# Where the last stage's inputs are stored: a ternary feed-forward kernel whose final reload of x gets more places in SBUF

## The chip, the cores and the metric

The kernel runs on one core of a Trainium2 chip. The metric is the device time of one execution in microseconds (us), the median of the runs of a kernel. A profiled execution has a time of its own and a span, from the first to the last instruction in the trace; instants below ("at 1038.7") are microseconds from the span's start. MB are millions of bytes; a block of x or of the output is 1.049 MB.

## The reference

x has 128 samples of 64 channels by 512 positions, in fp32 (16.78 MB). Each sample picks one of 200 matrices of 64 by 64; the picked matrix mixes the channels. Then a two-layer feed-forward network with ternary weights runs over the 512 positions of each of the 8192 rows, its output y is rounded to 15 levels with one scale for the whole tensor, and x is added.

```python
c = einsum('bct,bcd->bdt', x, weights[conditions])
W1q, W2q = ternarize(W1), ternarize(W2)     # alpha * sign(W) where |W| > 0.05 * max|W|
h = gelu(c @ W1q.T + b1)                    # 512 -> 2048
y = h @ W2q.T + b2                          # 2048 -> 512
scale = max(abs(y)) / 7 + 1e-8              # one number, over all of y
out = x + clip(round(y / scale), -7, 7) * scale
```

The scale needs the largest |y| of all blocks, so no output can be written before the last y is there.

## The kernel before

The rows are cut into 16 blocks (NB) of four pairs of samples: 128 partitions by 4 by 512, in fp32. A block n goes through 16 steps hc, one for each 128 of the 2048 hidden units. In a step, TensorE does eight matmuls of layer 1 into `ph` (`layer1`) and eight of layer 2 into the four accumulators `py0` to `py3` (`layer2`), the latter for the step two earlier (LAG). Activations are split in a high and a low fp32r part, so that each product is two matmuls. Between the layers ScalarE does the gelu into `hf` and rounds it to the high part, and VectorE subtracts to get the low part (`bend`, `split`).

The ternary weights rest in SBUF as fp8, `w1t` and `w2t`, one buffer each. GpSimd widens one step's share of them at a time to fp32r: `widen1` for the next step's layer 1, `widen2` for the layer 2 of the step before (`w1f`, `w2f`, three buffers each, pool `wide`). GpSimd also issues the gathers of the picked matrices (`fetch`, L172) and copies them into the block diagonals `diag` (`place`, L184), for the block after.

The kernel opens with the work on the weights: SP loads W1, x block 0 and W2; VectorE finds the largest |W1|, TensorE spreads it over the partitions by a transpose (`tops_delta_w`), VectorE makes masks and signs, TensorE transposes them. Until the first real matmul, TensorE does 64 matmuls `idle` on a tile of ones. Block 0 runs its two layers one after the other, in step with the preparation of W2 (L538 to L656); from block 1 the loop at L661 runs as above.

Storage: the pool `big` has 21 buffers of 8 KB a partition, for x blocks, their two parts, raw weights, masks, `w1t`, `w2t`, and the y of each block, which `result` (L433) takes out of PSUM. When the last block runs, 15 y are held, and the 16th gets a buffer when it is done.

All engines keep the program's order (`InOrder`, L43), and so does SP's queue of loads: a load that waits for its buffer holds up all loads after it. Loads of x are issued as two halves of 0.524 MB. The last stage needs x again. `load_x` is called for x0 and x1 in the last block (L675), for x2 at its end (in the buffer of `w1t`), and for x3 and x4 after it (L703; in the last block's parts). When the main loop's pools are closed (L727), a pool `last` takes their place with three x buffers for x5, x6 and x7, and x8 to x15 go into buffers of x and y that the last stage sets free (L734).

The last stage itself (L732 to L748), by half blocks: ScalarE rounds y into an int8 `q` (three buffers), VectorE writes q times scale plus x over y, GpSimd issues the write to `out`. Ahead of it stand the largest |y| of the last block and the scale (L708 to L724): for each j, VectorE takes y out of PSUM (`result`) and reduces it (`largest`); then one transpose spreads the maximum.

Of the kernel before, what the change touches and what calls it, by code (L numbers as in the profile page):

```python
# [25 lines left out]
F32 = mybir.dt.float32  # L26
BF16 = mybir.dt.bfloat16
F32R = mybir.dt.float32r
# [26 lines left out]
def tile_cond_ternary_ffn(  # L55
# [30 lines left out]
    const = ctx.enter_context(tc.tile_pool(name="const", bufs=1))  # L86
    big = ctx.enter_context(tc.tile_pool(name="big", bufs=21))
    gather = ctx.enter_context(tc.tile_pool(name="gather", bufs=2 * PAIRS))
    main = ctx.enter_context(ExitStack())
    hid = main.enter_context(tc.tile_pool(name="hid", bufs=3))  # L90
    wide = main.enter_context(tc.tile_pool(name="wide", bufs=3))
    ps_c = ctx.enter_context(tc.tile_pool(name="ps_c", bufs=2, space=PSUM))
# [5 lines left out]

    def load_x(n, pool=big, tag="big"):
        xt = pool.tile([P, PAIRS, T], F32, tag=tag, name=f"xt_{n}")  # L100
        for h in range(2):
            js = slice(h * PAIRS // 2, (h + 1) * PAIRS // 2)
            sp.dma_start(out=xt[:, js, :], in_=x_blk[n][:, js, :])
        return xt

    first = big.tile([P, 3, B], F32, tag="big", name="first")
    cond_i = first[:, 0, :].bitcast(I32)
    sp.dma_start(out=cond_i, in_=conditions.partition_broadcast(P))  # L110
# [8 lines left out]
    x_next = load_x(0)  # L119
    b1n = const.tile([NH, P], F32)  # L120
    sp.dma_start(out=b1n, in_=b1.rearrange("(k p) -> k p", p=P))
# [14 lines left out]
    make_identity(nc, ident_f)  # L136
    ones_b = const.tile([P, T], BF16)
    pool.memset(ones_b, 1.0)
# [10 lines left out]
    rows = const.tile([P, B // 2], I32)  # L149
    cond_f = first[:, 1, :]  # L150
    dve.tensor_copy(cond_f, cond_i)
    wrap = first[:, 2, :]
    dve.tensor_scalar(wrap, cond_f, 0.0, float(S), ALU.is_lt, ALU.mult)
    dve.tensor_tensor(cond_f, cond_f, wrap, ALU.add)
    dve.tensor_scalar(cond_f, cond_f, 0.0, float(S - 1), ALU.max, ALU.min)
    cond_2 = cond_f.rearrange("p (j two) -> p j two", two=2)
    for h in range(2):
        half = slice(h * C, (h + 1) * C)
        dve.tensor_scalar(
            rows[half, :], cond_2[half, :, h], float(C), chan_f[half, :], ALU.mult, ALU.add  # L160
        )
    table = weights.rearrange("s c d -> (s c) d")


    diag = []
    for j in range(PAIRS):
        wd = const.tile([P, P], F32, tag=f"diag{j}", name=f"diag{j}")
        pool.memset(wd, 0.0)
        diag.append(wd)

# [13 lines left out]
    def place(j, wg):  # L184
        for h in range(2):
            half = slice(h * C, (h + 1) * C)
            pool.tensor_copy(diag[j][half, h * D : (h + 1) * D], wg[half, :])

# [8 lines left out]
    def mix(xt, j, pc):  # L197

        for c in range(NT):
            pe.matmul(  # L200
                out=pc[:, c, :],
                lhsT=xt[:, j, c * P : (c + 1) * P],
                rhs=diag[j],
                start=True,
                stop=True,
            )
# [6 lines left out]

    w1t = big.tile([P, NH, NT, P], F8, tag="big", name="w1t")
    w2t = big.tile([P, NH, T], F8, tag="big", name="w2t")

    def spread(top1, out):

        wide_top = const.tile([P, P], F32, tag="wide_top", name=f"wide_{out.name}")
        dve.tensor_copy(wide_top, top1.to_broadcast([P, P]))  # L220
        tops = ps_c.tile([P, P], F32, tag="pc", name=f"tops_{out.name}")
        pe.transpose(tops, wide_top, ident_f)
        return tops

    def thresholds(w, top):

        top1 = const.tile([P, 1], F32, name=f"top1_{w}")
        dve.tensor_reduce(top1, top, AX.X, ALU.max)
        delta = const.tile([P, 1], F32, name=f"delta_{w}")
        tops = spread(top1, delta)  # L230
        yield
        dve.tensor_reduce(delta, tops, AX.X, ALU.max)
        dve.tensor_scalar(delta, delta, THRESHOLD, None, ALU.mult)
        minus = const.tile([P, 1], F32, name=f"minus_{w}")
        dve.tensor_scalar(minus, delta, -1.0, None, ALU.mult)
        yield delta, minus
# [44 lines left out]
    def flat(w):  # L281
        return w.rearrange("p a b -> p (a b)")
# [14 lines left out]

    idle = ps_h.tile([P, T], F32, tag="ph", name="idle")
    for _ in range(64):
        pe.matmul(out=idle, lhsT=ones_b[:, :P], rhs=ones_b, start=True, stop=True)  # L300
    for g in range(NG):
# [18 lines left out]

    find = thresholds("w1", top_1)
    next(find)
# [19 lines left out]
    def count1(g, number, first, final):  # L342
        for i in range(WCH // T):
            pe.matmul(
                out=number,
                lhsT=ones_b[:, :P],
                rhs=tern1[g][:, 0, i * T : (i + 1) * T],
                start=(first and i == 0),
                stop=(final and i == WCH // T - 1),
            )  # L350
# [34 lines left out]
    def widen1(n, hc):  # L385

        w = wide.tile([P, NT, P], F32R, tag="w1f", name=f"w1f_{n}_{hc}")
        pool.tensor_copy(w, w1t[:, hc])
        wide1[n, hc] = w

    def widen2(n, hc):
        w = wide.tile([P, T], F32R, tag="w2f", name=f"w2f_{n}_{hc}")
        pool.tensor_copy(w, w2t[:, hc])
        wide2[n, hc] = w
# [130 lines left out]
    def alpha_2():  # L525
# [10 lines left out]
        alpha[2] = alpha_of("w2", both[:, 0:1], both[:, 1:2])  # L536

    widen1(0, 0)  # L538

# [41 lines left out]
    fetched = []  # L581
    find = thresholds("w2", top_2)
    made = {}
# [35 lines left out]
    for hc in range(5, NH):  # L619
# [5 lines left out]
        behind(hc)  # L625
    turned = turn2(0, 1, signs2[0][:, 1, :])
    widen2(0, 0)
    widen2(0, 1)
# [9 lines left out]
    for hc in range(NH - LAG):  # L638
# [13 lines left out]
        if 8 <= hc < 8 + NG:  # L652
            sum2(hc - 8)
    cond[1] = two_next
    widen1(1, 0)
    widen2(0, NH - LAG)  # L656


    steps = [(n, hc) for n in range(NB) for hc in range(NH)]
    again = []  # L660
    for s in range(NH, len(steps)):  # L661
        n, hc = steps[s]
        if s + 1 < len(steps):
            widen1(*steps[s + 1])
        widen2(*steps[s + 1 - LAG])
        if n + 1 < NB:
            if hc == 0:
                x_next = load_x(n + 1)
                two_next = parts(n + 1)
                fetched = []  # L670
            if 2 <= hc < 2 + PAIRS:
                fetched.append(fetch(n + 1, hc - 2))
            if 7 <= hc < 7 + PAIRS:
                place(hc - 7, fetched[hc - 7])
        if n == NB - 1 and hc in (2, 3, NH - 1):  # L675
            again.append(load_x(len(again)))
        ph = ps_h.tile([P, BLK], F32, tag="ph", name=f"ph_{n}_{hc}")
        layer1(n, hc, ph)
        bend(
            n,  # L680
            hc,
            ph,
            [hid.tile([P, BLK], F32R, tag=f"h{k}", name=f"h{k}_{n}_{hc}") for k in range(2)],
            hid.tile([P, BLK], F32, tag="hf", bufs=2, name=f"hf_{n}_{hc}"),
        )
        if n + 1 < NB and 8 <= hc < 8 + PAIRS:
# [14 lines left out]
    n = NB - 1  # L701
    widen2(n, NH - 1)
    for _ in range(2):  # L703
        again.append(load_x(len(again)))
    dve.tensor_reduce(
        ymax[:, NB, 0:1], ymax[:, : NB - 1].rearrange("p n j -> p (n j)"), AX.X, ALU.max
    )
    for j in range(PAIRS):  # L708
        for hc in range(NH - 1 - LAG, NH):
            layer2(n, hc, [j])  # L710
        result(n, j)
        largest(n, j)

# [5 lines left out]
    scale = const.tile([P, 1], F32, name="scale")  # L719
    tops = spread(ymax1, scale)  # L720
    dve.tensor_reduce(scale, tops, AX.X, ALU.max)
# [4 lines left out]

    main.close()  # L727
    last = ctx.enter_context(tc.tile_pool(name="last", bufs=3))
    for _ in range(3):
        again.append(load_x(len(again), last, "xt"))  # L730
    AHEAD = len(again)
    for n in range(NB):  # L732

        while len(again) < min(AHEAD + 3 * n // 2, NB):  # L734
            again.append(load_x(len(again)))
        xf = again[n].rearrange("p j t -> p (j t)")
        yf = ys[n].rearrange("p j t -> p (j t)")
        for h in range(2):
            half = slice(h * PAIRS * T // 2, (h + 1) * PAIRS * T // 2)
            js = slice(h * PAIRS // 2, (h + 1) * PAIRS // 2)  # L740


            q = last.tile([P, PAIRS * T // 2], I8, tag="q", name=f"q_{n}_{h}")
            act.activation(q, yf[:, half], AF.Identity, scale=inverse)
            dve.scalar_tensor_tensor(
                yf[:, half], q, scale, xf[:, half], ALU.mult, ALU.add
            )
            pool.dma_start(out=out_blk[n][:, js, :], in_=ys[n][:, js, :])  # L748

# [33 lines left out]
```

## Time and profile before

| | us |
|---|---|
| median of 3 runs (range) | 1110.41 (1109.86 to 1111.0) |
| profiled execution | 1111.39 |
| its span | 1109.5 |
| TensorE busy | 1024.4 (92% of the span) |
| VectorE, ScalarE, GpSimd busy | 398.7, 471.2, 474.1 |
| DMA moved | 62.01 MB |

The shares are means over three stages with different limits: the opening until about 72, the blocks until 1035.5, where TensorE is busy nearly all the time, and the last stage, where TensorE has nothing to do. A change to the last stage is to be read from the rows of that stretch.

### The profile page before, as it was taken

To read this page: it belongs to the slowest core of one execution; us is meant where nothing else is said; L and a number is where in the kernel's file an instruction comes from. 1 tells how busy PE (TensorE), PEld (TensorE's weight loads), DVE (VectorE), ACT (ScalarE), POOL (GpSimd) and SP (SyncE) were. 2 spreads that over 40 slices of the span, in tenths; PEclk is the share of its full clock that TensorE was granted. 3 is DMA by queue.
4 is the path that set the end of the run, shared out by engine and by line. 5 is a ranking of instruction groups with operands and counts; after the bars stand their busy time and mean duration, and the time that the engine had idled before them with its cause. 6 is when DMAs were issued, how large, how long until landed. Compare 5 with 4: busy or idle time off the path is not lost.

```text
span 1109.5 us, 13261 instructions
## 1 busy us (share of the span) xinstructions
PE 1024.4 (92%) x4832; PEld 839.9 (76%) x4832; DVE 398.7 (36%) x545; ACT 471.2 (42%) x648; POOL 474.1 (43%) x757
## 2 busy tenths in 40 slices
PE   8989999999999999999999999999999999999300
PEld 4768788888888888888888888888888888888200
DVE  6965323232322323232322323232323223231753
ACT  6855333434344343343343433434333334333551
POOL 3756435343443535343444435353434435333331
PEclk9999999999999999999999999999999999999755
DMA  9113100100101000100101000100101000021899
GB/s 331 71 39 114 43 1 6 38 6 1 40 4 40 5 1 6 38 5 1 42 2 40 4 1 6 38 6 1 43 1 41 3 1 5 1 77 38 320 415 362
DMA packets 28672, 62.01 MB, mean 56 GB/s; under 512 B 2736, under 2 KB 2880, under 8 KB 28608
## 3 DMA queue, kind: packets, MB, share of 16 engines
q1 hardware_dynamic: 21952, 42.28, 11.0%
q0 software_dynamic: 6656, 18.88, 4.4%
q8 instruction: 39, 0.64, 0.2%
q14 instruction: 25, 0.20, 0.1%
HBM read 44.38 MB, written 16.78 MB: 55 GB/s over the span
## 4 chain that ended last, share of the span: by engine, by line
PE 88%; DMA 4%; DVE 3%; issue 2%; POOL 1%; ACT 1%; SPq 0%; POOLq 0%; ACTq 0%; DVEq 0%
PE py L51 42%; PE ph L51 41%; PE pc L51 5%; DMA out<-y 3%; DMA nat<-in_L_ffn_W 1%; DVE tern L51 1%; DMA xt<-in_x 1%; DVE y L51 1%; POOL diag L51 0%; PE pt L51 0%; POOL out L51 0%; DVE ymax L51 0%; ACT ring L51 0%; ACT h L51 0%; DVE x L51 0%
## 5 line engine op out<-in xcount | busy, mean ns | idle before, releaser
L51 PE MATMUL py<-w2f,h 128*128 128x512 f32 x2048 | 516.9, 394 | 2.8 <-ACT ring L51 1.9
L51 PE MATMUL ph<-x,w1f 128*128 128x512 f32 (+1 forms) x2056 | 507.1, 389 | 3.3 <-POOL w1f L51 3.3
L51 PEld LDWEIGHTS ph<-x,w1f 128*128 128x128 f32 x2056 | 384.1, 188 | 84.5 <-POOL w1f L51 4.9
L51 PEld LDWEIGHTS py<-w2f,h 128*128 128x128 f32 x2048 | 378.5, 188 | 85.6 <-DVE y L51 5.6
L51 ACT ACTIVATE hf<-ph,b1t,alpha_w 128x512 f32<-128x512 f32 x240 | 187.2, 780 | 554.7 <-PE ph L51 554.7
L51 DVE TENSOR_TENSOR h<-hf,h 128x512 fp32r<-128x512 f32 x240 | 166.1, 692 | 650.8 <-ACT h L51 650.8
L51 POOL CAST w2f<-w2t 128x512 fp32r<-128x512 fp8e4 x256 | 184.9, 723 | 358.3 <-PE py L51 347.4
L51 POOL CAST w1f<-w1t 128x512 fp32r<-128x512 fp8e4 x256 | 163.5, 639 | 192.5 <-PE ph L51 179.1
L51 ACT CAST h<-hf 128x512 fp32r<-128x512 f32 x240 | 148.8, 620 | 7.6
L51 PEld LDWEIGHTS pc<-diag,xt 128*128 128x128 f32 x512 | 66.2, 191 | 4.5
L51 POOL DMA_INDIRECT wg<-in_L_cond_weights,rows x64 | 62.8, 982 | 13.1 <-issue 5.3
L51 PE MATMUL pc<-diag,xt 128*128 128x128 f32 x512 | 67.0, 274 | 0.0
L51 DVE SCALAR_TENSOR_TENSOR y<-q,scale,xt 128x1024 f32<-128x1024 int8 x32 | 39.4, 1281 | 26.3 <-DMA xt<-in_x 25.0
L51 ACT ACTIVATE q<-y,inverse 128x1024 int8<-128x1024 f32 x32 | 36.0, 1145 | 29.4 <-DVE y L51 19.9
L51 DVE TENSOR_TENSOR x<-pc,x 128x512 fp32r<-128x512 f32 x64 | 43.5, 683 | 9.1 <-ACT x L51 9.1
L51 POOL DMA_DIRECT2D out<-y x32 | 23.3, 728 | 54.4 <-DVE y L51 38.7
L51 DVE SCALAR_TENSOR_TENSOR y<-py,alpha_w,b2b 128x512 f32<-128x512 f32 x64 | 43.8, 743 | 0.7 <-PE py L51 0.5
L51 DVE TENSOR_REDUCE ymax<-y 128x1 f32<-128x512 f32 x64 | 39.6, 676 | 0.1
L51 ACT CAST x<-pc 128x512 fp32r<-128x512 f32 x64 | 37.1, 581 | 3.9 <-PE pc L51 3.9
L51 POOL COPY diag<-wg 64x64 f32<-64x64 f32 x128 | 33.8, 264 | 8.2 <-DMA wg<-in_L_cond_weights,rows 4.4
L51 DVE TENSOR_REDUCE top<-nat 128x1 f32<-128x2048 f32 x8 | 18.2, 2280 | 3.9 <-DMA nat<-in_L_ffn_W 3.9
L51 PE MATMUL idle<-ones_b 128*128 128x512 bf16 x64 | 16.4, 425 | 2.2 <-POOL ones_b L51 2.2
(73 smaller groups left out, 171.9 us busy)
## 6 DMA issues: line engine op xcount, KB each, us to landing
xt<-in_x SPq DMA_DIRECT2D x64, 512.0 KB, 4.9
out<-y POOLq DMA_DIRECT2D x32, 512.0 KB, 13.1
nat<-in_L_ffn_W SPq DMA_DIRECT2D x8, 1024.0 KB, 13.1
wg<-in_L_cond_weights,rows POOLq DMA_INDIRECT x64, 2.4
b2b<-in_L_ffn_b SPq DMA_DIRECT2D x1, 256.0 KB, 13.5
first<-in_itok_B SPq DMA_DIRECT2D x1, 64.0 KB, 3.5
b1n<-in_L_ffn_b SPq DMA_DIRECT2D x1, 8.0 KB, 11.1
```

Of the source, the lines that this page charges most:

```text
L51: return lambda *args, **kw: self._tc.keep_in_program_order(make(*args, **kw))
```

## The change

It gives the reload of x more places, and frees what it needs for that:

- `last` and the closing of the main pools are gone. One pool `half` of six half-size buffers (4 KB a partition) replaces `hid` and `wide`: one each for `w1f`, `w2f` and `hf`, of two slots each, and three for the two parts of h. After the main loop the six take the halves of x7, x8 and x9.
- `w1f` and `w2f` have two slots from block 1 on instead of three. For block 0 the slots are in `big`: four of `w1f0` and four of `w2f0`. The last `widen2` goes into a slot of `w1f`.
- `big` has 22 buffers. The last y takes none: it gets its alpha and bias in place in PSUM, is reduced there and rounded from there, and its output is written over x15.
- x0, x1, x2 are loaded at steps 0, 1 and 2 of the last block. x3 goes into `w1t` and x4 into `w2t`, a quarter (0.262 MB) each time four steps' weights have been widened for the last time (`lend`). x5 and x6 follow after the loop, then the six halves. x10 to x15 go into buffers that the last stage frees.
- `q` lies in `diag`, which becomes one tile: two half-block slots instead of three buffers.
- Small tiles move into others: `b1n` and the spread maxima into `first`, `junk` and `diag`; `ones_b` shrinks to 128 by 128, and the `idle` matmuls read the first 512 elements of `junk`, which GpSimd sets to 1. `gather` has four buffers instead of eight.

```diff
-    big = ctx.enter_context(tc.tile_pool(name="big", bufs=21))
-    gather = ctx.enter_context(tc.tile_pool(name="gather", bufs=2 * PAIRS))
-    hid = main.enter_context(tc.tile_pool(name="hid", bufs=3))
-    wide = main.enter_context(tc.tile_pool(name="wide", bufs=3))
+    big = ctx.enter_context(tc.tile_pool(name="big", bufs=22))
+    gather = ctx.enter_context(tc.tile_pool(name="gather", bufs=PAIRS))
+    half = ctx.enter_context(tc.tile_pool(name="half", bufs=6))
...
-    ones_b = const.tile([P, T], BF16)
+    ones_b = const.tile([P, P], BF16)
...
-    for j in range(PAIRS):
-        wd = const.tile([P, P], F32, tag=f"diag{j}", name=f"diag{j}")
-        pool.memset(wd, 0.0)
+    diag = const.tile([P, PAIRS, P], F32)
+    pool.memset(diag, 0.0)
...
+    pool.memset(above[:, :T], 1.0)
     for _ in range(64):
-        pe.matmul(out=idle, lhsT=ones_b[:, :P], rhs=ones_b, start=True, stop=True)
+        pe.matmul(out=idle, lhsT=ones_b, rhs=above[:, :T], start=True, stop=True)
...
     def widen1(n, hc):
-        w = wide.tile([P, NT, P], F32R, tag="w1f", name=f"w1f_{n}_{hc}")
+        w = w1f0[:, hc % 4] if n == 0 else w1f[:, hc % 2]
         pool.tensor_copy(w, w1t[:, hc])
...
     def widen2(n, hc):
-        w = wide.tile([P, T], F32R, tag="w2f", name=f"w2f_{n}_{hc}")
+        if n == 0 and hc < NH - LAG:
+            w = w2f0[:, hc % 4]
+        elif n == NB - 1 and hc == NH - 1:
+            w = w1f[:, 0].rearrange("p c h -> p (c h)")
+        else:
+            w = w2f[:, hc % 2]
         pool.tensor_copy(w, w2t[:, hc])
...
+    w1f = half.tile([P, 2, NT, P], F32R, tag="half", name="w1f")
+    w2f = half.tile([P, 2, T], F32R, tag="half", name="w2f")
+    hf = half.tile([P, 2, BLK], F32, tag="half", name="hf")
...
+    dying = [flat(t).bitcast(F32).rearrange("p (j t) -> p j t", j=PAIRS) for t in (w1t_f, w2t)]
+
+    def lend(t, n, hc):
+        if n == NB - 1 and hc % (NH // PAIRS) == NH // PAIRS - 1:
+            j = hc // (NH // PAIRS)
+            sp.dma_start(out=dying[t][:, j, :], in_=x_blk[3 + t][:, j, :])
...
             widen1(*steps[s + 1])
+            lend(0, *steps[s + 1])
         widen2(*steps[s + 1 - LAG])
+        lend(1, *steps[s + 1 - LAG])
...
-        if n == NB - 1 and hc in (2, 3, NH - 1):
-            again.append(load_x(len(again)))
+        if n == NB - 1 and hc < 3:
+            again.append(load_x(hc))
...
     widen2(n, NH - 1)
+    lend(1, n, NH - 1)
+    again += [t for t in dying]
     for _ in range(2):
         again.append(load_x(len(again)))
...
-        result(n, j)
-        largest(n, j)
+        y = ypsum[n][j]
+        dve.scalar_tensor_tensor(y, y, alpha[2], b2b, ALU.mult, ALU.add)
+        dve.tensor_reduce(
+            ymax[:, n, j : j + 1], y, AX.X, ALU.max, apply_absolute_value=True
+        )
...
-    main.close()
-    last = ctx.enter_context(tc.tile_pool(name="last", bufs=3))
-    for _ in range(3):
-        again.append(load_x(len(again), last, "xt"))
+    for i in range(6):
+        m, h = len(again) + i // 2, i % 2
+        xt = half.tile([P, PAIRS // 2, T], F32, tag="half", name=f"xt_{m}_{h}")
+        sp.dma_start(out=xt, in_=x_blk[m][:, pair_of_pairs(h), :])
+        halves.append(xt)
...
-            q = last.tile([P, PAIRS * T // 2], I8, tag="q", name=f"q_{n}_{h}")
+            q = quant[:, h * PAIRS // 2 : (h + 1) * PAIRS // 2, :]
+            if n < NB - 1:
+                y = res = ys[n][:, pair_of_pairs(h), :]
+                act.activation(flat(q), flat(y), AF.Identity, scale=inverse)
+                dve.scalar_tensor_tensor(
+                    flat(y), flat(q), scale, flat(xs[n][h]), ALU.mult, ALU.add
+                )
+            else:
+                res = xs[n][h]
+                for k in range(PAIRS // 2):
+                    y = ypsum[n][h * PAIRS // 2 + k]
+                    act.activation(q[:, k, :], y, AF.Identity, scale=inverse)
+                    dve.scalar_tensor_tensor(
+                        res[:, k, :], q[:, k, :], scale, res[:, k, :], ALU.mult, ALU.add
+                    )
```

## The prediction

> **What bounds the kernel now.** I read the page's slices first, then busy time in stretches cut at the last stage's events, then the timeline there, then the waits.
>
> ```profile
> PE   8989999999999999999999999999999999999300
> DMA  9113100100101000100101000100101000021899
> ...
> GB/s 331 71 39 114 43 1 6 38 6 1 40 4 40 5 1 6 38 5 1 42 2 40 4 1 6 38 6 1 43 1 41 3 1 5 1 77 38 320 415 362
> ```
>
> TensorE fills the span up to slice 37 (27.7 us each), then has nothing; DMA is nearly empty until then and full afterwards. The kernel is bound by TensorE for 1035 us and by DMA for the last 74. What can be loaded while TensorE works costs nothing; what is left for the end costs its bytes.
>
> ```profile
> 1024.50:1029.50 5.00, 5.00 (x23) 3.83 (x21) 0.69 (x1) 2.20 (x4) 0.72 (x1) 1.00 0.17 21
> 1029.50:1035.50 6.00, 5.08 (x21) 3.67 (x20) 4.81 (x8) 0.59 (x1) 0.00 (x0) 1.00 0.90 333
> 1035.50:1037.50 2.00, 0.00 (x0) 0.00 (x0) 1.86 (x5) 0.00 (x0) 0.00 (x0) 1.00 0.41 51
> 1037.50:1045.00 7.50, 0.30 (x1) 0.14 (x1) 5.68 (x8) 6.25 (x7) 2.24 (x3) 0.53 1.05 392
> 1045.00:1102.00 57.00, 0.00 (x0) 0.00 (x0) 33.04 (x27) 29.73 (x27) 19.63 (x28) 0.50 1.04 415
> 1102.60:1104.60 2.00, 0.00 (x0) 0.00 (x0) 1.28 (x1) 0.00 (x0) 0.10 (x1) 0.50 1.01 408
> 1104.60:1106.00 1.40, 0.00 (x0) 0.00 (x0) 0.00 (x0) 0.00 (x0) 0.72 (x1) 0.50 0.11 41
> 1106.00:1107.50 1.50, 0.00 (x0) 0.00 (x0) 0.00 (x0) 0.00 (x0) 0.00 (x0) 0.50 0.86 330
> ```
>
> These are busy times of the engines in stretches; the last two columns are the DMA share and GB/s. x3 and x4 move from 1029.8 to 1035.3, then comes a hole of 2 us, because x5 to x7 are issued only at 1035.5, behind the last matmul. Reads alone run at 392, reads beside writes at 415, and the writes alone after the last x at 1102.6 at 408 (around 395 in whole microseconds of the DMA records). At 1104.6 there is another hole of 1.4 us: the last output waits for the last x.
>
> ```profile
> 1041.51 0.77 POOL L51 DMA_DIRECT2D out<-y  x1 [13.84 <-DVE y L51]
> 1103.07 1.28 DVE L51 SCALAR_TENSOR_TENSOR y<-q,scale,xt 128x1024 f32<-128x1024 int8 x1 [1.40 <-DMA xt<-in_x]
> 1104.66 0.72 POOL L51 DMA_DIRECT2D out<-y  x1 [1.96 <-DVE y L51]
> DVE y L51 <- DMA xt<-in_x: 25.0, 11, 2.5
> ```
>
> Three lines of the timeline and one of the waits (total, times, longest). The first output is issued at 1041.5 and moves from 1045.06; the last moves until 1107.45, and the span ends 2.1 later. VectorE waits 25 us for x. In the DMA records of 1050 to 1100, x gets 0.1435 MB/us and the outputs 0.272, whose packets are 2 and 4 KB.
>
> The sum closes. At 1037.5, 11 blocks of x and 16 of output are to move, 28.31 MB: 7.5 us at 0.392 take 2.94, the remaining 25.37 at 0.415 take 61.1, and the hole 1.4: 1107.5, as measured.
>
> **The last stage after the change.** x0 to x2 and seven of the eight quarters of x3 and x4 move during the last block, where the slices show DMA at two tenths at most. The loads hold up each other on SP's queue, not an engine. The rest, in order:
>
> - The last quarter (0.262 MB) waits for the last `widen2`. `w2f` 14 now waits for layer 2 of step 12, which ends at 1026.7; its cast (0.72) and the next give 1028.3. Then x5 and x6 (2.097 MB), free when layer 1 of step 15 ends at 1028.5: five issues of 0.45 us. Issue to first byte is 2 us (1027.7 to 1029.8), so DMA starts at 1030.4.
> - The first half of x7 waits for `hf`, read last by VectorE at 1030.8. The others wait for the last j's matmuls at 1034.6 to 1035.4; their bytes are due from 1036.7. DMA has work until 1037.6, so the hole closes.
> - Until the first output, at 1045.06 before and 1045.3 now (see below), 14.9 us at 0.392 could move 5.84 MB; queued are 0.262 + 2.097 + 3.146 = 5.51. x10, freed by VectorE at about 1042.6, starts at 1044.6. I take 0.2 MB of x10 as done by 1045.3.
> - Then 6.09 MB of x10 to x15 at 0.1435 take 42.4 us, to 1087.7. Beside them 11.5 MB are written; the remaining 5.24 at 0.395 take 13.3: 1101.0. The last residual is done by 1090, with eight writes still queued, so the second hole goes. With 2.1 behind it the span would end at 1103.1, 6.4 earlier.
>
> Of this, 5.05 are two blocks at 0.415; the two holes give 3.4; the last quarter, the 0.6 us later start and slower lone writes take back the rest.
>
> The Trainium skill, in "DMA: Bandwidth & Descriptors" (Specifications), gives about 358 GB/s as a core's limit to HBM. By that the 28.31 MB would take 79 us where they took 70; the trace's 415 decides. If lone writes fell to 358, the last 5.24 MB would take 14.6 and the gain be 5.1.
>
> **Parts of the change off that sum.**
>
> - y in PSUM: `largest` reads PSUM instead of SBUF. The same reduction of 128x512 from PSUM took 678 ns (`count<-number`), from SBUF 676: nothing. The write into PSUM by VectorE has no row; nearest is the same operation with PSUM source, 743 ns. Four on the path to the scale: I take +0.2 us in all, bounds -0.2 and +0.6. The outputs start later by it; loads hide only part.
> - `q` with two slots: the rounding (1145 ns) waits for the residual (1281) two halves earlier, so a half takes at least (1145 + 1281)/2 = 1.21 us plus hand-over, about 1.3, where 1.2 is seen. A half drains in 0.524/0.272 = 1.93. Cost nothing, covered by the queued writes; uncovered it would be 32 x 0.1 = 3.
> - For the last block, four smaller roundings and residuals, some 0.8 each, lie before 1091, with writes queued until 1101.
> - The same 62 MB, on SP eight quarters for four halves: four more issues of some 0.5 us, in the last block, where SP has time.
> - GpSimd's casts from block 1 on: in a step TensorE takes two times 1.81 us. With two slots `w1f` is free when layer 1 of two steps before ends, 5.4 us before its use. Worst case behind it: own cast 0.61, the other's 0.72, a gather 0.98, a copy pair 0.52, together 2.9. 2.5 us of cover are left: nothing. For block 0 four slots only loosen it; there TensorE's waits are for gelu and for casts held up by `diag` copies. Bounds -1 and +1.
> - `gather` with four buffers: a gather of the next block follows its slot's copies by 11 steps. Nothing. The 22nd buffer and the two slot tiles in `big` only shift who inherits which buffer; in the built program no inherited release is later than what the instruction waits for anyway. Nothing.
>
> **The opening.** Here the change adds a wait. The first `idle` matmul now needs the memset of `junk`, which GpSimd issues last. The timeline before:
>
> ```profile
> 1.61 0.52 POOL L51 MEMSET ones_b<- 128x512 bf16 x1
> 2.19 16.44 PE L51 MATMUL idle<-ones_b 128*128 128x512 bf16 x64 [2.19 <-POOL ones_b L51]
> 2.60 0.63 POOL L51 MEMSET diag<- 128x128 f32 x4
> 19.50 0.33 PE L51 MATMUL tops_delta_w<-ident_f,wide_delta_w 128*128 128x128 f32 x1 [0.87 <-DVE wide_delta_w L51]
> ```
>
> `ones_b` saves 0.3; `ones_f`, the channel numbers, `diag` (0.5 for 512 elements) and `junk` (0.5) then stand ahead: about 3.3 instead of 2.19. Behind the idle matmuls on TensorE is `tops_delta_w`, for which VectorE waits with all of the ternary chain; TensorE was 0.87 us early. The first 12 matmuls came at 0.427 us, up to 7.2, the rest at 0.224. If the clock rises at 7.2 again, 9 are done by then and 55 x 0.224 end at 19.5: no delay. The Trainium skill ("TensorE: Matmul & The Clock Gate", What's actually happening) says the clock rises after a busy window of 3.4 us that runs free of the kernel. A later first matmul can then miss a window, with the rise up to 10.1: 16 slow ones, 48 x 0.224, end at 20.9, and everything is 1.4 later. The trace fits such windows (rise at 7.2, half clock from 72.0 to 75.5). I take +0.3, between 0 and 1.4.
>
> **Sum**, against the profile's own span: 1109.5 - 6.4 + 0.3 = 1103.4. The profiled execution took 1111.39, 0.98 over the median of 1110.41; I carry the difference of -6.1 to the median: 1104.3.
>
> **The rivals.**
>
> - GpSimd stalls TensorE (slower). With the third slots, reserve is lost in the 8 steps of each of 14 blocks that also gather or copy: 112 steps. TensorE has no wait for `w1f` in the trace after the first step of block 1; but GpSimd's waits for TensorE show that it takes each slot as it comes. If the 2.5 us do not hold, because a gather or copy waits too, each 0.1 us costs 11.2: 1115.5. It decides from 6.1/112 = 0.054 us a step.
> - The lone writes stay at the 0.272 they have beside reads, as if their own queue were the limit: 5.24/0.272 = 19.3 instead of 13.3, so 1110.3, no change. Against it stand the 408 of 1102.6 to 1104.6; for it only that this row is 2 us long.
> - The change does not do what it says: x5 to x9 are not early, since SP's in-order queue holds them behind the last quarter, which waits for GpSimd's last cast. Late by d, DMA idles up to d; with d = 3, 1107.3. Against it: that cast needs only step 12's matmuls.
>
> **How the numbers follow.** A measurement here tells 0.2%, 2.2 us, from no change. My forecast, 0.72, spans 1101.9 (lone writes at 408, no delay of the opening) to 1105.9 (+1.4 in the opening, +0.2 of slower writes). A smaller gain (358, or late loads) 0.15: to 1108. No change 0.06, slower 0.07. The range for 8 in 10 is 1101.9 to 1107.6.
>
> **What would show it.** Right: two more blocks in before the scale; no DMA hole between 1030.5 and 1100; last x at about 1088 and last residual by 1091, then some 11 us of writes alone near 395; VectorE's wait for x well under 25 us; blocks of 61.9 us as now. Wrong: waits of TensorE for `w1f` or `w2f` after block 0, the first TensorE work after `idle` later than 20, a DMA share under 0.9 before 1100, or rounding and residual taking turns at over 1.8 us a half.

## The result, and the profile after

| us | before | after |
|---|---|---|
| median (range), 4 runs each | 1110.65 (1109.86 to 1111.0) | 1103.04 (1102.26 to 1104.07) |
| profiled execution | 1111.39 | 1102.89 |
| its span | 1109.5 | 1101.0 |
| end of the last layer 1 (start of its row + 8 x 0.227) | 1028.46 | 1026.53 |
| from there to the end of the span | 81.04 | 74.47 |

The ratio of the times is 0.9936 (0.9923 to 0.9948). The kernel is 7.6 us faster; 1104.3 was predicted. TensorE's clock is halved for 3.41 us at about 72 in some executions of one and the same kernel and not in others (the first experiments below); the profiled execution of before has such a stretch and that of after has none, and mainly for this reason 1.93 of the 8.5 us between the spans lie ahead of the last stage. The last stage itself gives 81.04 - 74.47 = 6.57.

The page's slices of after: TensorE's busy tenths, the granted clock, the DMA share and GB/s.

```profile
PE   8989999999999999999999999999999999999500
...
PEclk9999999999999999999999999999999999999855
DMA  9214001000101001000001001000001001111799
GB/s 329 75 39 153 5 1 44 1 5 5 37 5 39 6 1 43 1 4 8 34 4 39 6 2 42 1 4 12 30 5 39 5 3 41 39 58 39 264 413 371
```

The bytes that were 77 and 38 GB/s in two slices ahead of the last stage of before are now spread over 41, 39, 58 and 39: quarters and blocks that arrive while TensorE works. What is left behind TensorE is as dense as before, and shorter.

The last stage in stretches (busy us and count of PE, PEld, DVE, ACT and POOL, then clock, DMA share, GB/s):

```profile
1028.30:1033.40 5.10, 4.93 (x20) 3.65 (x20) 4.53 (x8) 0.00 (x0) 0.00 (x0) 1.00 0.98 356
1033.40:1036.00 2.60, 0.33 (x2) 0.14 (x1) 2.09 (x5) 0.00 (x0) 0.00 (x0) 1.00 1.05 406
1036.00:1043.30 7.30, 0.11 (x1) 0.00 (x0) 5.75 (x8) 5.80 (x6) 2.24 (x3) 0.56 1.06 393
1043.30:1085.60 42.30, 0.00 (x0) 0.00 (x0) 33.04 (x28) 31.06 (x29) 18.14 (x25) 0.50 1.03 413
1085.60:1087.50 1.90, 0.00 (x0) 0.00 (x0) 0.62 (x1) 0.00 (x0) 0.72 (x1) 0.50 1.01 410
1087.50:1098.80 11.30, 0.00 (x0) 0.00 (x0) 1.41 (x2) 0.00 (x0) 2.18 (x3) 0.50 0.96 388
1098.80:1101.00 2.20, 0.00 (x0) 0.00 (x0) 0.00 (x0) 0.00 (x0) 0.00 (x0) 0.50 0.01 4
```

Both holes of before are gone: in no stretch from 1028.3 to 1098.8 is the share under 0.96. The last row but one is the writes alone, 11.3 us of them (of x, less than 0.01 MB moves there).

The timeline there, and what VectorE waited for (total us, times, longest):

```profile
1039.70 0.77 POOL L51 DMA_DIRECT2D out<-y  x1 [13.41 <-DVE y L51]
1040.63 4.27 SPq L51 DMA_DIRECT2D xt<-in_x  x4
1088.40 1.41 DVE L51 SCALAR_TENSOR_TENSOR xt<-diag,scale,xt 128x512 f32<-128x512 int8 x2 [2.18 <-DMA xt<-in_x]
1090.11 0.72 POOL L51 DMA_DIRECT2D out<-xt  x1 [0.36 <-DVE xt L51]
```

```profile
DVE y L51 <- DMA xt<-in_x: 6.9, 3, 2.7
...
DVE xt L51 <- DMA xt<-in_x: 4.3, 2, 2.2
```

The last output is issued at 1090.11 and its bytes still have to queue until 1098.8; before, it was issued into an empty queue. VectorE's wait for x falls from 25.0 to 11.2 us, and none of it is on the path that sets the end.

The opening of after, and TensorE's waits for the casts of layer 1:

```profile
3.32 15.33 PE L51 MATMUL idle<-junk,ones_b 128*128 128x512 bf16 x64 [3.32 <-POOL junk L51]
19.63 0.33 PE L51 MATMUL tops_delta_w<-ident_f,first 128*128 128x128 f32 x1 [0.98 <-DVE first L51]
```

```profile
PE ph L51 <- POOL w1f L51: 3.3, 3, 1.7
```

The idle matmuls start 1.13 later and end no later (18.65 and 18.63): the clock rises at 6.10 us where in before it rose at 7.19, so that more of them run at the full clock. The three waits for `w1f` lie in block 0 as before; for `w2f` there is none.

### The profile page after: what moved, and what is told of

Same layout as the page of the kernel before. It is cut to its first block, busy times and chain, and to the rows that moved or that the text cites. A ratio compares the mean times of both kernels' runs of the same rounds, so it can differ in the third digit from the quotient of the medians.

```text
span 1101.0 us, 13309 instructions
## 1 busy us (share of the span) xinstructions
PE 1021.5 (93%) x4832; PEld 838.6 (76%) x4832; DVE 399.3 (36%) x547; ACT 472.1 (43%) x650; POOL 468.3 (43%) x755
## 4 chain that ended last, share of the span: by engine, by line
PE 88%; DMA 4%; ACT 3%; DVE 2%; POOL 1%; issue 1%; SPq 0%; POOLq 0%; ACTq 0%; DVEq 0%
PE py L51 42%; PE ph L51 40%; PE pc L51 5%; DMA out<-y 3%; DMA nat<-in_L_ffn_W 1%; DVE y L51 1%; ACT diag L51 1%; ACT junk L51 1%; POOL diag L51 0%; POOL w1f L51 0%; DVE top L51 0%; PE pt L51 0%; DMA wg<-in_L_cond_weights,rows 0%; POOL wg L51 0%; DVE ymax L51 0%
## 5 line engine op out<-in xcount | busy, mean ns | idle before, releaser
L51 POOL CAST w2f<-w2t 128x512 fp32r<-128x512 fp8e4 x255 | 178.4, 701 | 359.2 <-PE py L51 335.8
L51 DVE SCALAR_TENSOR_TENSOR y<-py,alpha_w,b2b 128x512 f32<-128x512 f32 x60 | 40.8, 743 | 0.2 <-DVE alpha_w L51 0.2
L51 ACT ACTIVATE diag<-y,inverse 128x1024 int8<-128x1024 f32 x30 | 34.3, 1147 | 13.7 <-DVE inverse L51 8.8
L51 DVE TENSOR_REDUCE ymax<-y 128x1 f32<-128x512 f32 x60 | 36.8, 676 | 0.0
L51 DVE SCALAR_TENSOR_TENSOR y<-diag,scale,xt 128x1024 f32<-128x1024 int8 x26 | 32.4, 1282 | 8.4 <-DMA xt<-in_x 6.9
L51 PE MATMUL idle<-junk,ones_b 128*128 128x512 bf16 x64 | 15.3, 404 | 3.3 <-POOL junk L51 3.3
```

Of the source, the lines that this page charges most:

```text
L51: return lambda *args, **kw: self._tc.keep_in_program_order(make(*args, **kw))
```

## The experiments

**The stretch of half clock.** The first four kernels ask whether the 1.93 us of the opening belong to the change. `fill` adds seven matmuls of 128x512 in TensorE's idle times in layer 2 of block 0, in before and in after; `before_late` gives before the later start of the idle matmuls; `after_early` gives after the earlier one.

```diff
 before_fill, after_fill
-        layer2(0, hc)
+        if hc == 0:
+            fill = ps_c.tile([P, T], F32, tag="pc", name="fill")
+            for js, more in (([0], 5), ([1], 2), ([2, 3], 0)):
+                layer2(0, hc, js)
+                for _ in range(more):
+                    pe.matmul(out=fill, ...)
+        else:
+            layer2(0, hc)
 before_late: idle reads junk behind its memset
+    pool.memset(above[:, :T], 1.0)
 after_early: the same memset directly behind that of ones_b
+    pool.memset(junk[:, 0, :T], 1.0)
```

before_fill: 

> The kernel before, with seven 128x512 bf16 matmuls whose result nobody reads, put on TensorE where it stands idle in layer 2 of block 0 (about 69.0 to 70.2 and 71.0 to 71.6). Theory A (the 1.9 us by which TensorE ends earlier after the change are the stretch at half clock from 72.0 to 75.5, which follows these idle times): no half clock after the opening, TensorE's last layer-1 matmul 1.7 us earlier, 1108.9. Theory B (something else in the opening of the changed kernel saves 1.9 us): as before, 1110.6, or later by up to 0.3 through the extra matmuls.

before_late: 

> The kernel before, with the idle matmuls reading a tile that GpSimd sets to 1 last, as in the change: they start at about 3.3 instead of 2.2. Nothing else is changed. Theory A1 (the clock's windows run free of the kernel; whether one of them is idle enough is chance): half clock around 72 in some runs and not in others, for this kernel as for the one before; medians within 1 us of each other. Theory A2 (the later start itself moves the windows): never half clock there, 1108.7. Rival of the prediction's own term: a missed window in the opening, up to 1.4 us later.

after_early: 

> The changed kernel, with the memset that the idle matmuls wait for moved to second place on GpSimd, so that they start at about 2.4 instead of 3.3. Theory A1: as the changed kernel, 1103.0, some runs with half clock around 72 and some without. Theory A2: half clock around 72 in every run, 1104.8.

after_fill: 

> The changed kernel with the same seven extra matmuls in the idle times of layer 2 of block 0. Theory A: no half clock there in any run, so the spans lie close together at the lower end of the changed kernel's: 1102.4. Theory B: no gain, 1103.0 or 0.2 more.

Measured, beside 25 runs of before with a median of 1110.01: before_fill 1110.16 (1109.57 to 1110.53, ratio 0.9998), before_late 1110.82 (1109.16 to 1111.52, 1.0002), after_early 1102.86 (1102.15 to 1104.04, 0.9935), after_fill 1103.01 (1101.95 to 1103.08, 0.9931). The stretch of 72.00 to 75.50 in before, before_late, before_fill and after (the clock is the third number from the right):

```profile
72.00:75.50 3.50, 3.50 (x10) 2.73 (x9) 3.50 (x4) 1.51 (x3) 0.87 (x1) 0.51 0.00 0
```

```profile
72.00:75.50 3.50, 3.50 (x10) 2.69 (x9) 3.50 (x4) 1.36 (x3) 1.09 (x1) 0.52 0.00 0
```

```profile
72.00:75.50 3.50, 3.50 (x25) 2.87 (x24) 3.50 (x4) 1.89 (x4) 1.40 (x1) 1.00 0.00 0
```

```profile
72.00:75.50 3.50, 3.50 (x26) 2.87 (x25) 3.50 (x4) 1.89 (x4) 0.00 (x0) 1.00 0.00 0
```

Of before's 25 runs, 7 lie at 1110.9 to 1112.1 with a mean clock of 0.966, and 18 at 1109.2 to 1110.25 with 0.967 to 0.969: one kernel, two groups, with medians 1.7 us apart. With the fillers none of 13 runs is over 1110.53. The change is not needed for the stretch to come or to go: theory A2 falls with before_late, whose profile has the stretch, and B with before_fill, whose last layer 1 ends at 1026.35 (2.1 earlier). Removing it does not move before's median, because most of its runs have none; the 1108.9 and 1102.4 expected with fillers were not met for that reason.

What decides in which executions the stretch comes can be read from the 13 profiled executions of this case. The steps of the clock lie whole multiples of 3.413 us apart (the rise and the drop at 72 by 64.85, 19 times, in all four that have it; the rise and the drop after TensorE's work by 301 or 302 times in those that don't), so each trace can be cut into windows of that length, counted from its own rise of the clock. Three of the windows (the second number is TensorE's busy time): the one ahead of the drop in before, the least busy one near 70 in after, and in whole_fill (an experiment below), which has the fillers and the same rise at 7.19 as before:

```profile
68.63:72.04 3.41, 1.54 (x6) 0.68 (x5) 2.94 (x4) 3.35 (x5) 1.30 (x1) 1.00 0.02 5
```

```profile
67.54:70.95 3.41, 2.15 (x14) 1.03 (x13) 1.98 (x3) 3.33 (x6) 2.22 (x4) 1.00 0.00 0
```

```profile
68.63:72.04 3.41, 3.04 (x12) 1.28 (x12) 2.94 (x4) 3.35 (x5) 1.86 (x2) 1.00 0.02 5
```

In the four executions with the stretch (before, before_late, after_whole, after_twice) TensorE is busy for 1.54 to 1.68 us of the window ahead of it; in every other window between the rise and 140, in all 13, for 1.72 or more. In those four the clock had risen at 6.51 to 7.34, so that one window takes in the first idle time of layer 2 of block 0 and at least part of the second; in the four others without fillers it rose at 5.81, 6.10, 8.04 and 9.11, and no window takes in that much. So theory A1 holds: the stretch depends on how an execution falls against the clock's windows, not on the change. Between the two filled kernels, where the stretch cannot fall at 72, the change gives 1110.16 - 1103.01 = 7.15 us.

**Same room, filled later, still under TensorE.** All eight quarters are issued behind the last `widen2` in the program.

```diff
-        if n == NB - 1 and hc % (NH // PAIRS) == NH // PAIRS - 1:
-            j = hc // (NH // PAIRS)
-            sp.dma_start(out=dying[t][:, j, :], in_=x_blk[3 + t][:, j, :])
+        if (n, hc, t) == (NB - 1, NH - 1, 1):
+            for u in range(2):
+                for j in range(PAIRS):
+                    sp.dma_start(out=dying[u][:, j, :], in_=x_blk[3 + u][:, j, :])
```

> The changed kernel, but all eight quarters of x3 and x4 are issued only behind the last widen2 instead of one by one during the last block: the room is the same, it is filled later. Seven quarters (7 x 0.262 = 1.835 MB) move from the time in which TensorE works into the last stage. Theory (the end is set by the bytes that are left when the last stage begins, at the 0.413 MB/us of reads beside writes): +1.835/0.413 = +4.4 us on 1103.0, so 1107.4 (1106.8 to 1108.2), with no hole in the DMA slices. Rival (the gain is the closed holes and the earlier queueing alone, bytes are hidden behind the writes): 1103 to 1104.

Measured: 1104.37 (1102.82 to 1105.05). A miss, and the edit's, not the theory's: the bytes did not move. Two stretches of after_whole:

```profile
1022.00:1024.00 2.00, 2.00 (x11) 1.65 (x10) 0.69 (x1) 0.40 (x1) 0.72 (x1) 1.00 0.62 169
1024.00:1026.00 2.00, 2.00 (x11) 1.65 (x10) 0.00 (x0) 1.38 (x2) 0.00 (x0) 1.00 0.92 320
```

The last quarter of x3 and the first three of x4 moved between 1022 and 1026, with TensorE fully busy, and those of x3 before them earlier still. A load waits for the last reader of its own piece of buffer, not for its place in the program; only a waiting load ahead of it on SP's queue holds it. So the bytes stayed under TensorE, and the tail behind the last layer 1 is 75.29 (after: 74.47). The profiled execution has the half-clock stretch (0.60 to 0.70 in the single microseconds of 72 to 76), which accounts for most of the rest of its 2.3 us of span. The kernels without the fillers can have that stretch in some of their runs, which blurs their medians by up to 1.7 us; for them the tail is the safer measure.

**The same, held for good.** In the filled kernel the quarters are issued behind x5 and x6, which do wait for the last layer 1.

```diff
     for _ in range(2):
         again.append(load_x(len(again)))
+    for u in range(2):
+        for j in range(PAIRS):
+            sp.dma_start(out=dying[u][:, j, :], in_=x_blk[3 + u][:, j, :])
```

> The changed kernel with the seven extra matmuls (1103.0), but the eight quarters of x3 and x4 are issued behind x5 and x6, which wait for the last layer 1; this time their place in SP's in-order queue holds them. Seven quarters, 1.835 MB, leave the time of TensorE and come into the last stage. Theory (bytes left at the end of TensorE's work set the time, at 0.413 MB/us): +4.4, less up to 0.7 because the changed kernel's DMA engines end unevenly: 1106.7 to 1107.5. Rival (these bytes would be hidden anyway, as the run that moved them by a few us suggests): 1103 to 1103.5.

Measured: 1108.38 (1106.57 to 1109.69), +5.4, and 0.9 over the expected range; the rival's 1103 is refuted. Five of its 14 runs, 1106.6 to 1106.9, lie where the bytes alone put them; nine lie at 1108.2 to 1109.7. The profiled one (1108.61) shows what is on top, in the timeline and in the stretches of its end:

```profile
1100.41 1.42 DVE L51 SCALAR_TENSOR_TENSOR xt<-diag,scale,xt 128x512 f32<-128x512 int8 x2 [2.19 <-DMA xt<-in_x]
1102.13 0.73 POOL L51 DMA_DIRECT2D out<-xt  x1 [2.88 <-DVE xt L51]
```

```profile
1101.00:1102.00 1.00, 0.00 (x0) 0.00 (x0) 0.83 (x2) 0.00 (x0) 0.00 (x0) 0.50 0.45 180
1102.00:1103.00 1.00, 0.00 (x0) 0.00 (x0) 0.00 (x0) 0.00 (x0) 0.73 (x1) 0.50 0.02 8
1103.00:1105.00 2.00, 0.00 (x0) 0.00 (x0) 0.00 (x0) 0.00 (x0) 0.00 (x0) 0.50 0.68 262
```

With 1.8 MB more of x to fetch, the last x comes when the writes have run dry: DMA share 0.45, then 0.02, the hole that before had at 1104.6. Whether the runs at 1106.6 escape it, no profile shows.

**y of the last block in SBUF.**

```diff
-    for _ in range(2):
-        again.append(load_x(len(again)))
+    again.append(load_x(len(again)))
...
-        dve.scalar_tensor_tensor(y, y, alpha[2], b2b, ALU.mult, ALU.add)
-        dve.tensor_reduce(ymax[:, n, j : j + 1], y, ...)
+        result(n, j)
+        largest(n, j)
...
-            if n < NB - 1:
+            if n < NB:
```

> The changed kernel with the y of the last block in SBUF again, so that one block of x fewer (x5 alone) is loaded behind the last layer 1 and the six halves take x6 to x8. Bytes alone: one block more in the last stage, 1.049/0.413 = +2.5 us, less 0.1 for the scale path without PSUM writes: 1105.4. Theory with the hole: queued ahead of the first output are 0.262 + 1.049 + 3.146 = 4.46 MB, which at 0.392 from 1028.3 are done at 1039.7, and the next block waits for a residual and starts at 1042.6 while the first output moves from 1041.8: a hole of about 2.1 us opens, so +4.6 in all: 1107.5, with DMA share under 0.5 between 1039.7 and 1041.8. Rival (y in PSUM costs on the path as much as it frees): 1103.

Measured: 1104.89 (1104.68 to 1105.23), +1.9: nearer to the bytes alone (1105.4) than to 1107.5. The hole comes, elsewhere than expected: x5 alone does not last until the halves, whose slots the last matmuls read.

```profile
1032.00:1034.00 2.00, 1.49 (x7) 0.91 (x5) 1.97 (x4) 0.00 (x0) 0.00 (x0) 1.00 0.47 149
```

After moves 383 GB/s in these 2 us, so the hole is 0.47 MB; up to 1044 the two kernels differ by 1.03 MB in all, one block: the hole is part of that block's 2.5 us, not on top of it, and it was counted twice in the expectation. The tail grows by 2.05.

**The same room, started late.** First by reversing the order of the loads, then with a load of 512 bytes ahead of them that waits for `ymax1`.

```diff
 after_held
...
+    for i in reversed(range(6)):
+        m, h = len(again) + i // 2, i % 2
+        sp.dma_start(out=halves[i], in_=x_blk[m][:, pair_of_pairs(h), :])
+    for m in (5, 6):
+        ...
 held_fill (x5 and x6 likewise taken out of their place)
...
+    sp.dma_start(out=ymax[:, n, 0:1], in_=x_blk[0][:, 0, 0:1])
+    for m in (5, 6):
+        for h in range(2):
+            js = pair_of_pairs(h)
+            sp.dma_start(out=again[m][:, js, :], in_=x_blk[m][:, js, :])
```

> The changed kernel with the same room, but x5 to x9 are issued in another order, the half whose slot is read by the last matmul first, so that SP's in-order queue holds all of them until about 1035.3. Theory (what counts is when the bytes start, not how many buffers there are): DMA has only the last quarter of x4 between 1028.3 and 1037.3; the start of x5 moves from 1028.6 to 1037.3, less nothing else: +7.5 to +8.5 us, 1110.5 to 1111.5, as slow as the kernel before. Rival (the number of blocks ahead of the scale sets the end, the DMA catches up behind): at most +1, 1104.

Measured: 1106.84 (1106.25 to 1108.17), +3.8 (the tail +3.9), half of what was expected. SP issued the first half at 1029.21, right behind the last reader of `hf`: the reversed order still had that slot first, it seems because the pool hands out its slots in the order in which they are first written. One half moved early, the rest from about 1035 instead of 1037.3, and at 1044 only 1.9 MB were missing, not 3.2.

> The changed kernel with the seven extra matmuls (1103.0) and all of its room, but x5 to x9 stand on SP's queue behind a load of 512 bytes that waits for the reduction ymax1 at 1035.2, so their bytes start at about 1037.3 instead of 1028.6. The changed kernel moves 347 to 406 GB/s from 1028 to 1037.3, some 3.5 MB, of which only the last quarter is left: a deficit of 3.2 MB. Theory (when bytes start is what counts): 3.2/0.413 = +7.8, less up to 0.7: 1110.1 to 1110.9, no faster than before with the same buffers. Rival (the number of blocks in before the scale decides): at most 1104.

Measured: 1111.49 (1110.86 to 1112.09), +8.5, 0.6 over the expected range; the ratio to before is 1.0008 (1.0001 to 1.0014). Stretches of held_fill:

```profile
1028.30:1037.30 9.00, 5.43 (x21) 3.73 (x21) 7.13 (x15) 0.31 (x1) 0.00 (x0) 0.91 0.05 8
...
1043.30:1103.00 59.70, 0.00 (x0) 0.00 (x0) 34.09 (x28) 31.12 (x29) 20.37 (x28) 0.50 1.03 411
```

All of the change's buffers, and nothing gained: 9 us with DMA at 0.05 cost what the two blocks had brought. It is the start of the bytes that counts.

**The ledger.** In all, 33.55 MB of x and outputs must move for the last stage. From the GB/s of the stretches: what is in when the last layer 1 ends (whole blocks and quarters), what moves in the 16 us behind it, and what is then left; the time for the rest is the tail less 16 and less the last 2.1 us.

| kernel | in, MB | in 16 us | left | us for it | MB/us |
|---|---|---|---|---|---|
| before | 3.15 | 4.94 | 25.46 | 62.9 | 0.405 |
| after | 4.98 | 5.67 | 22.90 | 56.4 | 0.406 |
| after_y_sbuf | 4.98 | 4.93 | 23.64 | 58.4 | 0.405 |
| after_held | 4.98 | 3.93 | 24.64 | 60.3 | 0.409 |
| whole_fill | 3.15 | 5.47 | 24.93 | 62.1 | 0.401 |
| held_fill | 4.98 | 2.12 | 26.45 | 65.2 | 0.406 |
| q1_fill (below) | 4.98 | 5.55 | 23.02 | 75.9 | 0.303 |

Six kernels whose tails differ by 8.8 us agree to 2% in one rate. That is 1.2 us in 60, about as much as the hole at the end of before and of whole_fill, so the ledger cannot tell such a hole. The seventh shows the other bound.

**An engine as the bound: one slot for `q`.**

```diff
-            q = quant[:, h * PAIRS // 2 : (h + 1) * PAIRS // 2, :]
+            q = quant[:, : PAIRS // 2, :]
```

> The changed kernel with the seven extra matmuls (1103.0), with one slot for q instead of two. Rounding and residual take turns: 1.145 + 1.281 and two hand-overs, 2.5 to 2.6 us a half. 30 halves of SBUF and the last block's four smaller pairs end at about 1037 + 30 x 2.55 + 7 = 1120, the last output then needs about 0.8 to issue, 2 to start, 1.3 to move, and 2.1 follow: a span of 1126, 1128 by the clock of the runs (1125 to 1130). Rival (a half drains in 1.27 us, TensorE's end and DMA still set the time; the engines catch up behind the queue): 1103.

Measured: 1122.41 (1122.36 to 1122.43), +19.4 where +25 was expected. Its timeline and two stretches:

```profile
1050.58 1.28 DVE L51 SCALAR_TENSOR_TENSOR y<-diag,scale,xt 128x1024 f32<-128x1024 int8 x1 [1.22 <-ACT diag L51]
1051.90 1.15 ACT L51 ACTIVATE diag<-y,inverse 128x1024 int8<-128x1024 f32 x1 [1.35 <-DVE y L51]
1053.08 1.28 DVE L51 SCALAR_TENSOR_TENSOR y<-diag,scale,w1t 128x1024 f32<-128x1024 int8 x1 [1.22 <-ACT diag L51]
```

```profile
1044.00:1084.00 40.00, 0.00 (x0) 0.00 (x0) 20.53 (x17) 18.38 (x16) 11.63 (x16) 0.50 0.98 371
1084.00:1112.00 28.00, 0.00 (x0) 0.00 (x0) 14.47 (x12) 12.74 (x12) 8.00 (x11) 0.50 0.55 211
```

Rounding and residual take turns, 2.50 us a half, and from 1084 DMA is half idle: 0.524/2.50 = 210 GB/s, just what the row shows. Most of the 5.6 us of error are the last block's pairs (7 us allowed, 3.6 taken, from 1111.9 to 1115.5) and the last output, into an empty queue (4.7 from its issue to the end, 6.2 allowed). With two slots, after does a half in 1.25 us, and a half takes 1.27 to drain at 413: the two are almost level, but the engines start ahead of the writes.

**GpSimd's cover.** Every cast of blocks 1 to 15 twice.

```diff
-        pool.tensor_copy(w, w1t[:, hc])
+        for _ in range(2 if n else 1):
+            pool.tensor_copy(w, w1t[:, hc])
 widen2 likewise
```

> The changed kernel, where GpSimd makes every cast of w1f and w2f of blocks 1 to 15 twice (the second writes the same values again): 0.62 + 0.70 us more in each step of 3.6 us. Theory (two slots leave some 2.5 us of cover in the worst step, so doubling leaves about 1.2): 1103.0 to 1104, TensorE with no new waits for w1f or w2f. Rival (with two slots the casts are nearly late, the steps that also gather or copy spill): 112 steps at some 0.1 to 0.5 us, 1114 to 1160.

Measured: 1104.61 (1103.94 to 1106.34), +1.6, a little over the expected 1104. The costliest GpSimd groups of after_twice, its waits of TensorE and its load of the last quarter:

```profile
L51 POOL CAST w1f<-w1t 128x512 fp32r<-128x512 fp8e4 x496 | 351.1, 708 | 73.5 <-PE ph L51 42.6 <-ACT w1t L51 10.2
L51 POOL CAST w2f<-w2t 128x512 fp32r<-128x512 fp8e4 x494 | 326.0, 661 | 154.7 <-PE py L51 112.9 <-ACT w2t L51 25.1
```

```profile
PE ph L51 <- POOL w1f L51: 3.5, 4, 1.6
```

```profile
1029.69 0.33 SPq L51 DMA_DIRECT2D w2t<-in_x  x1
```

The casts take 677 us where after has 342, and TensorE has one wait more, of 0.2 us; its weight loads, which overlap the matmuls, have three more, of 2.2 us together. The last layer 1 ends at 1028.53, 0.5 later than in after_whole, whose profiled execution has the half-clock stretch as well. The tail is 75.97, +1.5: the last cast is late and the last quarter, with x5 and x6 behind it on SP's queue, is issued 1.16 behind the end of layer 1 where in after it is 0.21 ahead of it. In the steps themselves nothing is lost: from the third on, a block takes 61.87 us, as in after and in before. So even here GpSimd shows mainly through the start of DMA.

## Why the prediction was right, point by point

- **The last stage, -6.4:** measured -6.57. The bound was rightly the bytes left when TensorE ends, and the ledger shows it in six kernels. Its terms were off in both directions by up to 2 us, and that they cancel to 0.2 is in part luck. On before's time axis (after's + 1.93), the first load moves from 1029.2 instead of 1030.4, because it is 1.0 us from issue to first byte (1026.32 to 1027.29) and not 2. That term was misread from before: its DMA records have x3 moving from 1028.7 and not 1029.8, and no load packet starting between 1035.3 and 1036.5, a first hole of 1.2 us and not 2. The first x then comes at 356 GB/s for 5 us where 392 was taken. The first output moves from 1043.7 instead of 1045.3, because it is 2.1 us from issue to bytes and not 3.6. The last x is in at 1089.9 instead of 1087.7, since writes share the rate earlier and the last 0.09 MB of x take 4 us; the lone writes run at 406 to 418 GB/s while all DMA engines have work, not 395, and at 388 over the whole stretch with its uneven end. The last byte is at 1101.1, where 1101.0 was worked out. A sum of bytes forgives when each of them moves, as long as there is no hole.
- **358 GB/s by the Trainium skill** ("DMA: Bandwidth & Descriptors", Specifications): measured 413 to 417 for reads beside writes and 406 to 418 for writes alone. The row there is half of what two cores have together, and one core runs here. The trace decides, as the prediction let it; the term of 1.3 us for it falls.
- **y in PSUM, +0.2:** from the end of the last layer 1 to that of `inverse` after takes 10.29, before 10.16: +0.13. The write into PSUM takes 751 ns, 743 the one to SBUF; the largest |y| takes 691 ns from PSUM, 676 from SBUF. The 678 that stood for "nothing" is another reduction, a sum (`count<-number`); four times the two differences are 0.09.
- **Two slots of q, nothing:** 1.25 us a half, 1.3 predicted; q1_fill shows that the one slot less would have cost 19.4.
- **GpSimd's casts, nothing:** a block takes 61.87 us before and after, and where neither has the half-clock stretch, the last layer 1 ends at 1026.35 in before_fill and at 1026.17 in after_fill. after_twice doubles the casts in 240 steps, and it ends 0.5 us later than in after_whole. The rival by which each of 112 steps loses 0.1 us is refuted with room to spare.
- **The opening, +0.3:** here the sum was off by a little, and for a reason that it named. The idle matmuls of after took 15.33 us and delayed nothing. In the eight other kernels with the same opening and the same start (3.31 to 3.33) they took 15.30 to 16.82, and `tops_delta_w` came at 19.52 to 19.97, the latest in after_held, where the clock rose last, at 9.11. So the cost is 0 to 0.4 by how the execution falls, and 0 in the profiled one, which was luck. The windows of 3.4 us in "TensorE: Matmul & The Clock Gate" (What's actually happening) agree with this: in these nine the clock rose at 6.05 to 9.11, less than one window apart. The rise at 10.1 and the delay of 1.4 that they allow were not seen in any profile.
- **The carry to the median, -6.1:** the median moved by 7.6. The last stage gives 6.6 and the opening's 0.3 did not come. Between the filled kernels, where no profile has the half-clock stretch, the last stage gives 81.55 - 74.83 = 6.7, the earlier end of layer 1 0.2, and the medians differ by 7.15; the rest of 0.25 is less than the 1 us over which the runs of before_fill spread. That 7.6 was measured and not 7.15 fits the stretch, which can move a median of four runs by up to 1.7 us (1110.89 and 1111.0 of before lie at the edge of its group); which of these runs had it is not on record.
- **Lone writes at 272 GB/s** (no change): refuted by the row at 388 and by the 11.3 us it lasts.
- **Loads held behind the last quarter, d = 3:** the mechanism is real and was sized by held_fill: about 0.9 us for each us that the bytes start later. In after d is about zero: the last quarter is issued at 1026.32, x5 at 1026.75.

## What to carry to other kernels

Where DMA is idle under a bound engine and saturated behind it, a ledger of bytes (in before, moved in the first microseconds, left) tells the end to about a microsecond (2% of the tail here); count the start of the bytes and the holes, not the buffers. A load waits for the last reader of its own slot and for what waits ahead of it on its queue: its place in the program alone does not hold it, and dead weights, taken a quarter at a time, served here as well as a buffer. Before a difference of 1 to 2 us is explained, look at the runs of one and the same kernel for two groups, and at the granted clock for a stretch that only one of the profiles has.

## What was not expected of the hardware

- A stretch of half clock of 3.41 us, long after the opening, comes in some executions and not in others, and costs about 1.7 us. In all four profiled executions that have it, it begins 64.85 us after the clock has risen, 19 times 3.41, behind a window of that length in which TensorE was busy for 49% or less; no window with 50% or more was followed by one. No single gap in it was long: in before TensorE waits 1.27 and 0.59 us. With seven more matmuls there, none of the 18 runs of before_fill and after_fill lies in the group that has it. The busy times are those of the profile, which models the ends of matmuls, and no run here varied them around the half.
- In whole_fill the runs fall in two groups with medians 2.1 us apart and no stretch in the profile. The hole at its end explains the profiled one; what decides between the groups stays open.
- Outputs of 4 KB packets and x of 2 KB packets share the rate almost two to one (272 and 143 GB/s in before), and either alone reaches nearly the sum: 392 for reads, 410 for writes.
